# Two adapter layers with roles: orders and buffers of the first pair, of the changes of phase, of the left-overs and of the last pair

## The chip, the cores and the metric

The kernel runs on one core of one Trainium2 chip. The metric is the device time of one execution in microseconds (us), shown for several runs by its median. The profile is that of one further execution.

A core has a matrix engine (TensorE, PE in the profile; its weight loads are PEld), VectorE (DVE), ScalarE (ACT), GpSimd (POOL) and SyncE (SP), which here only issues transfers. Each engine works through its own list of instructions in order. Transfers between the main memory and the on-chip memory run on 16 DMA engines; they are issued from the list of SP or of ACT. TensorE writes into PSUM banks, which the other engines read.

## The reference

128 samples of 128 rows and 1024 columns (`x`) each have a role, drawn as 1 or 2 of three. Two layers follow one another, each with a set of weights for each role:

```python
h = jnp.einsum('bsh,bhk->bsk', hidden_states, W_down[role]) + b_down[role][:, None, :]
h = jax.nn.gelu(h, approximate=False)
u = jnp.einsum('bsk,bkh->bsh', h, W_up[role]) + b_up[role][:, None, :]
y = hidden_states + u
# mean and variance of y over its 1024 columns
return (y - mean) * jax.lax.rsqrt(var + LN_EPS) * gamma[role] + beta[role]
```

The inner width is 512. All data is float32.

## The kernel before

**Pairs, left-overs and phases.** At the start the kernel sorts the samples by role on the chip and takes two samples of one role as a pair: 63 pairs, and one item with the two samples that are left over, which may have different roles. There are four phases: down and up of the first layer (phases 0 and 1), down and up of the second (phases 2 and 3). A phase works through all 64 items; the left-over item comes after 31 pairs (`left_over_at`, L668). The results of a down phase (`hd`) and of the first layer (`mid`) go through the main memory.

**Seven products a pair.** The two samples of a pair stand above each other as a 2 by 2 block matrix, and so do the weights; the product is made from seven block products (`s1` to `s7`, L445 to L472) instead of eight. This takes sums of blocks of the activations (`winograd_sums`, L397, four instructions on GpSimd) and of the weights: T1 to T4. For phase 0 the weights are loaded as rows (`load_rows`, L142) and summed in place (`first_sum`, L162); for the other phases, class `Sums` makes the sums during phase 0 and stores them, and they are loaded block by block (B11, B21, T2, T1, T3, B22, T4) into the eight slots of `wall` as these come free. A left-over sample has the four products of the common method (`t1` to `t4`).

The products of one item add up in PSUM banks of three kinds, `b` (three banks), `a` (two) and `e` (three). Before the first product ACT writes the bias into a bank: the seed (`seeded`, L425). In a down phase ACT copies a bank into `h` (`begin`, L546), DVE adds another (`end`, L551) and ACT takes the GELU; the whole item is then stored by one transfer from ACT's list (`finish`, L557). In an up phase DVE adds the banks to `x` in place (L603, L608), the latter with a row sum; then `squares` (L624, on ACT with one small instruction on GpSimd), `scaled` (L634, DVE) and `stored` (L639) make the normalization and store the output from SP.

**Input of an item.** In a down phase each sample is loaded in four transfers of 128 KB (`quartered`, L383) and turned by a DVE transpose (L525) into the tile that TensorE reads. In an up phase `hq` comes in eight transfers of 64 KB (`load`, L569), and `x` of the residual in two of 512 KB (`load_rest`, L575).

**The order of the work.** All steps are put on a list with a time in slots by `at` (L661), and the instructions are issued in the order of these times; this fixes the order within each engine, and nothing more. An item takes seven slots, which is seven products. `base` is 7 times the item's number; the times of a class (`LOAD`, `REST`, `PREPARE`, `SEED`) and of its steps count from it. So the products of an item lie at 0, 2, ... 12, and those of two neighbours alternate. What a step waits for, beside the order, are data, buffers and the semaphores of the transfers, which are reused in turn.

**Buffers.** Tiles come from rings: `q` (four of 1024 columns: x of a down phase, `hq` and outputs of an up phase), `h` (two of 1024), `t` and `s` (three each). A new tile of a ring waits for the readers and transfers of the one that stood there before.

**The ends.** While the first weights are loaded, TensorE runs products of zeros (`zeros`, L269) into banks that nobody reads.

Of the kernel before, what the change touches and what calls it, by code (L numbers as in the profile page):

```python
# [19 lines left out]
P = 128  # L20
# [6 lines left out]
def kernel(  # L27
# [114 lines left out]
    def load_rows(k, place, engine, kind):  # L142
        w = layers[0][0]
        role = reg(role_of, place, [kind], R - 1)
        for q in range(NQ):
            src = w[ds(role, 1), ds(q * H // NQ + k * P, P), :]
            engine.dma_start(
                rows_of[k][ts(q, SQ), place].rearrange("p j h c -> p j (h c)"),
                src.rearrange("o (j i) c -> i (o j) c", i=SQ),
            )  # L150
# [123 lines left out]
    zeros("b")  # L274

# [80 lines left out]
    zeros("bbeee")  # L356
    for _ in range(4):
        zeros("bbb")
# [38 lines left out]
    def winograd_sums(dst, a):  # L397


        half = a.shape[2] // 2  # L400
        a11, a12, a21, a22 = (a[:, i, ts(k, half)] for i in range(2) for k in range(2))
        nc.gpsimd.tensor_tensor(dst[:, 1], a11, a21, ALU.subtract)  # L402
        nc.gpsimd.tensor_tensor(a21, a21, a22, ALU.add)
        nc.gpsimd.tensor_tensor(dst[:, 0], a21, a11, ALU.subtract)  # L404
        nc.gpsimd.tensor_tensor(dst[:, 2], a12, dst[:, 0], ALU.subtract)
# [26 lines left out]
    def item_products(item, cols):  # L432
# [9 lines left out]
        if n < NPAIR:  # L442
# [32 lines left out]
            times = (0, 2, 4, 1, 6.5, 6, 8) if item.early else range(0, 14, 2)  # L475
# [5 lines left out]
        for s in range(2):  # L481
# [18 lines left out]
            steps.append((2.5 * s - 4, lambda s=s, r=r: seed("b", (s, "b"), r)))  # L500
# [3 lines left out]
    class Down:  # L504
        LOAD, REST, PREPARE, SEED = -11.9, -11.8, -8.8, -4
# [6 lines left out]
        def load(self):  # L512
# [4 lines left out]
            quartered(self.xq, x_of(self.layer, self.n, ENG.SP))  # L517

        def load_rest(self):
            pass  # L520

        def prepare(self):
            self.a = flat("t", 3, "xT" + self.tag).rearrange("p (s j c) -> p s j c", s=2, c=P)
            for s in range(2):
# [3 lines left out]
                )  # L528
            self.sums = None
            if self.n < NPAIR:  # L530
# [3 lines left out]
                winograd_sums(self.sums, self.a)  # L534
# [5 lines left out]
        def first(self):  # L540
            self.h = flat("h", 2, "h" + self.tag, K * 2).rearrange("p (s n) -> p s n", s=2)

        def part(self, s, k):
            return self.h[:, s, ts(k, K // 2)]
# [12 lines left out]
        def finish(self):  # L557
            at = 12.5
            return [(at, lambda: nc.scalar.dma_start(hd[self.n].rearrange("s p n -> p s n"), self.h))]

    class Up:
        LOAD, REST, PREPARE, SEED = -11.5, -7, -5.5, -4
# [6 lines left out]
        def load(self):  # L569
            self.hq = flat("q", 4, "hq" + self.tag, H).rearrange(  # L570
                "p (s a c) -> p s a c", s=2, a=NQ
            )
            quartered([self.hq[:, s] for s in range(2)], [hd[self.n][s] for s in range(2)])
# [6 lines left out]
        def prepare(self):  # L580
            both = flat("s", 3, "hT" + self.tag, 1792)
            self.a = both[:, 0:1024].rearrange("p (s j c) -> p s j c", s=2, c=P)
            for s in range(2):
                nc.vector.transpose(  # L584
                    self.a[:, s].rearrange("p j (a t) -> p j a t", t=SQ),
                    self.hq[:, s].rearrange("p a (j i) -> p j a i", i=SQ),
# [6 lines left out]
            self.stat = small.tile([P, 2, 2], F32, tag="stat", name="stat" + self.tag)  # L593
# [11 lines left out]
        def end(self, s, k, ps):  # L605

            y = self.part(s, k)
            nc.vector.scalar_tensor_tensor(  # L608
# [4 lines left out]

        def finish(self):
            steps = []
# [54 lines left out]
    for k, ph in enumerate(phases):  # L670
        for m, n in enumerate(sequence):
# [4 lines left out]
            def load(box=box, ph=ph, n=n, kind=kind, m=m):  # L676
                item = box["item"] = kind(ph, n)
                item.early = ph is phases[0] and m == 0
                if ph is phases[2] and m == 0:
                    item.SEED = -0.6  # L680
                if m == left_over_at + 1:
                    item.SEED = -1.5
                item.load()

            at(base + kind.LOAD, load)
            at(base + kind.REST, lambda box=box: box["item"].load_rest())
# [54 lines left out]
    at(-12, lambda: load_bias([0]))  # L741
    at(-12, lambda: load_rows(0, 0, nc.scalar, ENG.Activation))
    at(-10, lambda: subtract(slice(0, 1)))
    at(-11, lambda: load_rows(1, 0, nc.sync, ENG.SP))
    for i, name in enumerate(("T1", "T2", "T3", "T4")):
        at(-8 + i / 10, lambda name=name: first_sum(name, 0))
# [50 lines left out]
```

## Time and profile before

| what | value |
|---|---|
| runs shown, median (lowest to highest) | 3194.6 us (3193.3 to 3203.4) |
| profiled execution, its own time | 3197.4 us |
| its span, first to last instruction | 3195.3 us |
| mean granted TensorE clock | 0.994 |
| TensorE busy | 3131.9 us (98%) |
| VectorE, ScalarE, GpSimd busy | 1772.8, 1200.4, 1791.7 us |
| moved by DMA | 642.9 MB, mean 201 GB/s |
| first real product starts at | 28.7 us |
| last pass of the last product starts at | 3177.0 us |
| first product of phases 1, 2 starts at | 811.9, 1617.8 us |

A line of a timeline has the start in us, the duration in us, the engine, the line of the kernel, the operation, the tile written and the tiles read, and in brackets how long the engine had been idle and what ended that. A float32 product of the kernel is recorded as two passes for each weight block, so that `x8` is one block product of a down phase (4 weight blocks) and `x4` one of an up phase (2 blocks). In tile names `b`, `a` and `e` are the banks, `d` and `u` the kind of phase: `bu` is a `b` bank of an up phase. `xTd`, `Sd` and `hTu` are turned activations and their sums.

### The profile page before, as it was taken

Reading aid. Unit: us, or ns where it says so; the run is one execution under the profiler, and the core shown is the slowest. Engines: PE = TensorE matmul, PEld = TensorE weight load, DVE = VectorE, ACT = ScalarE, POOL = GpSimd, SP = SyncE. Lnnn points to the kernel's source line nnn. Section 1 sums busy time; section 2 is a strip of 40 time slices with the busy share of each in tenths; the row PEclk is TensorE's granted clock in tenths of the full one; section 3 lists DMA queues with packets and bytes.
Section 4 is the critical chain, followed back from the end, with each engine's and each line's share of the span. In section 5 each row is a group of like instructions: output and inputs, shape, how many; then the busy total and the mean of one; then the engine's idle time right before and its main releaser. Section 6 shows DMA issues by size and latency. Waiting matters only on the chain. (4 is left out here: it accounts for less than half of the span.)

```text
span 3195.3 us, 43864 instructions
## 1 busy us (share of the span) xinstructions
PE 3131.9 (98%) x10824; PEld 2054.7 (64%) x10824; DVE 1772.8 (55%) x2783; ACT 1200.4 (38%) x2824; POOL 1791.7 (56%) x1399
## 2 busy tenths in 40 slices
PE   9999999999999999999989999999999999999997
PEld 6888888888534444444468888888884444444443
DVE  3533333334477777777743323233226777778877
ACT  1222222222345454545432222222224555454554
POOL 3544444444467776777754343443435777677775
PEclk9999999999999999999999999999999999999999
DMA  6776777777787666767796444544458766666664
GB/s 162 214 209 202 209 205 207 209 207 218 248 255 221 215 213 209 219 215 214 222 268 174 128 134 127 146 135 129 134 178 292 243 213 221 220 208 224 212 223 165
DMA packets 445506, 642.88 MB, mean 201 GB/s; under 512 B 46417, under 2 KB 316242, under 8 KB 445266
## 3 DMA queue, kind: packets, MB, share of 16 engines
q1 hardware_dynamic: 405986, 560.12, 59.6%
q10 hardware_dynamic: 39280, 79.96, 6.9%
q8 instruction: 102, 1.67, 0.2%
q14 instruction: 138, 1.13, 0.1%
HBM read 405.54 MB, written 234.36 MB: 200 GB/s over the span
## 5 line engine op out<-in xcount | busy, mean ns | idle before, releaser
L411 PE MATMUL bu<-wall,hTu 128*128 (+1 forms) x2048 | 929.9, 596 | 22.1 <-DVE xu L603 14.2
L411 PEld LDWEIGHTS bu<-wall,hTu 128*128 128x128 f32 x2048 | 386.3, 191 | 522.8 <-issue 426.2
L402 POOL TENSOR_TENSOR Sd<-xTd 128x512 f32<-128x512 f32 x126 | 168.6, 1338 | 842.0 <-DVE xTd L525 827.3
L632 POOL TENSOR_TENSOR varu<-varu,mhalf 128x1 f32<-128x1 f32 x256 | 334.8, 1308 | 414.6 <-ACT varu L631 367.0
L525 DVE STREAM_TRANSPOSE xTd<-xqd 128x1024 f32<-128x1024 f32 x256 | 307.9, 1230 | 438.8 <-PE bd L411 230.7
L411 PE MATMUL bd<-wall,xTd 128*128 (+1 forms) x2080 | 491.7, 380 | 7.8 <-DVE hd L551 5.2
L635 DVE SCALAR_TENSOR_TENSOR ou<-xu,meanu,tables 128x1024 f32<-128x1024 f32 x256 | 328.8, 1284 | 302.7 <-ACT ou L630 300.5
L411 PE MATMUL eu<-wall,hTu 128*128 (+1 forms) x1040 | 490.1, 594 | 4.1 <-DMA wall<-B 3.8
L411 PE MATMUL bd<-wall,Sd 128*128 (+1 forms) x2016 | 478.0, 380 | 4.4 <-ACT hd L547 4.4
L411 PEld LDWEIGHTS bd<-wall,xTd 128*128 128x128 f32 x2080 | 394.8, 190 | 66.2 <-DVE hd L551 7.3
L411 PEld LDWEIGHTS bd<-wall,Sd 128*128 128x128 f32 x2016 | 383.6, 190 | 59.4 <-POOL Sd L404 3.3
L411 PEld LDWEIGHTS eu<-wall,hTu 128*128 128x128 f32 x1040 | 198.0, 191 | 253.9 <-issue 240.6
L552 ACT ACTIVATE hd<-hd 128x256 f32<-128x256 f32 x382 | 157.2, 416 | 490.0 <-DVE hd L551 489.7
L626 ACT ACTIVATE partu<-statu 128x2 f32<-128x2 f32 x256 | 52.1, 203 | 759.4 <-DVE xu L608 759.4
L643 POOL TENSOR_TENSOR ou<-ou,tables 128x1024 f32<-128x1024 f32 x128 | 301.3, 2354 | 1.2 <-DMA hqu<-hd 0.9
L630 ACT ACTIVATE ou<-xu,meanu 128x1024 f32<-128x1024 f32 x256 | 294.0, 1148 | 19.1 <-DMA mid<-ou 4.2
L411 PE MATMUL ed<-wall,xTd 128*128 (+1 forms) x1072 | 252.9, 379 | 0.0
L402 POOL TENSOR_TENSOR hTu<-hTu 128x256 f32<-128x256 f32 x126 | 204.3, 1621 | 79.5 <-DVE hTu L584 77.7
L411 PE MATMUL ed<-wall,Sd 128*128 (+1 forms) x1008 | 238.1, 379 | 0.0
L411 PE MATMUL ad<-wall,xTd 128*128 (+1 forms) x1008 | 238.1, 379 | 0.0
L411 PE MATMUL au<-wall,hTu 128*128 (+1 forms) x504 | 236.8, 592 | 0.0
L411 PEld LDWEIGHTS ed<-wall,xTd 128*128 128x128 f32 x1072 | 203.7, 190 | 28.1 <-ACT ou L630 0.2
(96 smaller groups left out, 3348.6 us busy)
## 6 DMA issues: line engine op xcount, KB each, us to landing
xqd<-in_x_dram SPq DMA_DIRECT2D x512, 128.0 KB, 3.0
hd<-hd ACTq DMA_DIRECT2D x128, 512.0 KB, 2.8
hqu<-hd SPq DMA_DIRECT2D x1024, 64.0 KB, 4.1
xu<-in_x_dram SPq DMA_DIRECT2D x128, 512.0 KB, 5.3
mid<-ou SPq DMA_DIRECT2D x128, 512.0 KB, 5.2
xqd<-mid SPq DMA_DIRECT2D x512, 128.0 KB, 3.5
xu<-mid SPq DMA_DIRECT2D x128, 512.0 KB, 5.8
out_dram<-ou SPq DMA_DIRECT2D x128, 512.0 KB, 4.9
```

Of the source, the lines that this page charges most:

```text
L402: nc.gpsimd.tensor_tensor(dst[:, 1], a11, a21, ALU.subtract)
L411: nc.tensor.matmul(ps[:, 0:cols], a[:, j], w.rhs(r, j, cols), start=start and j == 0, stop=j == n - 1, skip_group_check=True,)
L525: nc.vector.transpose(self.a[:, s].rearrange("p j (a t) -> p j a t", t=SQ), self.xq[s].rearrange("p a (j i) -> p j a i", i=SQ),)
L552: nc.scalar.activation(y, y, AF.Gelu)
L626: nc.scalar.mul(part, self.stat[:, s], -1.0 / H)
L630: nc.scalar.activation(box["o"], self.x[:, s], AF.Square, bias=m, accum_out=v)
L632: nc.gpsimd.tensor_tensor(v, v, mhalf[:, 0:1], ALU.pow)
L635: nc.vector.scalar_tensor_tensor(box["o"], self.x[:, s], box["m"][:, 0:1], row(self.ph.gamma), ALU.add, ALU.mult)
L643: nc.gpsimd.tensor_tensor(o, o, row(self.ph.beta), ALU.add)
```

## The change

- **First pair.** Sample by sample, x is loaded at slots -30 and -27. The first two quadrants of the first weight rows are issued by ACT, the other two by SP; of the second rows, SP issues two quadrants after the second sample and ACT two at slot -3, after the seeds. T1 is summed between the two transposes, and three of the four activation sums are made by DVE. The second and third product change places. There are 9 products of zeros instead of 18.
- **x in phase 0** is loaded 19 slots ahead of `base` (17.4 for the fourth item) instead of 11.9. Phase 2 keeps its times.
- **h by sample.** Two rings `h0` and `h1` of two tiles each, and one store for each sample, at slots 10.7 and 12.5 instead of one at 12.5.
- **hq.** The first three items of an up phase load it at slot -16 instead of -11.5, into the ring `q`; the later ones load it at -11.5 as before, into `h0` and `h1`.
- **Left-overs.** The second sample's seed and the next pair's seed move from slot -1.5 to -1.65.
- **Last pair.** Mean and variance come from DVE's `bn_stats` and `bn_aggr`, and the output is stored in four pieces of 256 KB from SP and ACT.

```diff
-    def load_rows(k, place, engine, kind):
+    def load_rows(k, place, engine, kind, quadrants=range(NQ)):
         w = layers[0][0]
         role = reg(role_of, place, [kind], R - 1)
-        for q in range(NQ):
+        for q in quadrants:
             src = w[ds(role, 1), ds(q * H // NQ + k * P, P), :]
...
-    zeros("b")
     iota_row, iota_col, ones, upper = f32(B), f32(1), f32(B), f32(B)
...
     place = gathered("place", wide_place, onehot)
-    zeros("bbeee")
-    for _ in range(4):
-        zeros("bbb")
+    zeros("bbbeeebbb")
...
-    def winograd_sums(dst, a):
+    def winograd_sums(dst, a, engine=nc.gpsimd):
...
         a11, a12, a21, a22 = (a[:, i, ts(k, half)] for i in range(2) for k in range(2))
-        nc.gpsimd.tensor_tensor(dst[:, 1], a11, a21, ALU.subtract)
-        nc.gpsimd.tensor_tensor(a21, a21, a22, ALU.add)
-        nc.gpsimd.tensor_tensor(dst[:, 0], a21, a11, ALU.subtract)
+        engine.tensor_tensor(dst[:, 1], a11, a21, ALU.subtract)
+        engine.tensor_tensor(a21, a21, a22, ALU.add)
+        engine.tensor_tensor(dst[:, 0], a21, a11, ALU.subtract)
         nc.gpsimd.tensor_tensor(dst[:, 2], a12, dst[:, 0], ALU.subtract)
...
-            times = (0, 2, 4, 1, 6.5, 6, 8) if item.early else range(0, 14, 2)
+            times = (0, 1, 4, 2, 6.5, 6, 8) if item.early else range(0, 14, 2)
             steps = list(zip(times, (s1, s2, s3, s4, s5, s6, s7)))
...
             steps += [(1.75 * s + 3.5 * i, f) for i, f in enumerate((t1, t2, t3, t4))]
-            steps.append((2.5 * s - 4, lambda s=s, r=r: seed("b", (s, "b"), r)))
+            steps.append(((-4, -1.65)[s], lambda s=s, r=r: seed("b", (s, "b"), r)))
             steps.append((1.5 * s + 0.5, lambda s=s, r=r: seed("e", (s, "e"), r)))
...
     class Down:
-        LOAD, REST, PREPARE, SEED = -11.9, -11.8, -8.8, -4
+        LOAD, PREPARE, SEED = -11.9, -8.8, -4
...
             ]
-            quartered(self.xq, x_of(self.layer, self.n, ENG.SP))
+            self.srcs = x_of(self.layer, self.n, ENG.SP)
+            quartered(self.xq[0:1], self.srcs[0:1])
         def load_rest(self):
-            pass
+            quartered(self.xq[1:2], self.srcs[1:2])
...
                 )
+                if s == 0 and self.early:
+                    first_sum("T1", 0)
             self.sums = None
...
                 )
-                winograd_sums(self.sums, self.a)
+                winograd_sums(self.sums, self.a, nc.vector if self.early else nc.gpsimd)
             set_places(self, [ENG.PE, ENG.Activation])
...
         def first(self):
-            self.h = flat("h", 2, "h" + self.tag, K * 2).rearrange("p (s n) -> p s n", s=2)
+            self.h = [flat(f"h{s}", 2, f"h{self.tag}_{s}", K) for s in range(2)]
         def part(self, s, k):
-            return self.h[:, s, ts(k, K // 2)]
+            return self.h[s][:, ts(k, K // 2)]
...
         def finish(self):
-            at = 12.5
-            return [(at, lambda: nc.scalar.dma_start(hd[self.n].rearrange("s p n -> p s n"), self.h))]
+            return [
+                (t, lambda s=s: nc.scalar.dma_start(hd[self.n][s], self.h[s]))
+                for s, t in enumerate((10.7, 12.5))
+            ]
     class Up:
-        LOAD, REST, PREPARE, SEED = -11.5, -7, -5.5, -4
+        LOAD, PREPARE, SEED = -11.5, -5.5, -4
...
         def load(self):
-            self.hq = flat("q", 4, "hq" + self.tag, H).rearrange(
-                "p (s a c) -> p s a c", s=2, a=NQ
-            )
-            quartered([self.hq[:, s] for s in range(2)], [hd[self.n][s] for s in range(2)])
+            if self.m < 3:
+                hq = flat("q", 4, "hq" + self.tag, H)
+                self.hq = [hq[:, ts(s, K)] for s in range(2)]
+            else:
+                self.hq = [flat(f"h{s}", 2, f"hq{self.tag}_{s}", K) for s in range(2)]
+            self.hq = [t.rearrange("p (a c) -> p a c", a=NQ) for t in self.hq]
+            quartered(self.hq, [hd[self.n][s] for s in range(2)])
...
                     self.a[:, s].rearrange("p j (a t) -> p j a t", t=SQ),
-                    self.hq[:, s].rearrange("p a (j i) -> p j a i", i=SQ),
+                    self.hq[s].rearrange("p a (j i) -> p j a i", i=SQ),
                 )
...
             set_places(self, [ENG.PE, ENG.DVE, ENG.Pool, ENG.Activation])
-            self.stat = small.tile([P, 2, 2], F32, tag="stat", name="stat" + self.tag)
+            if self.last:
+                self.stat = const.tile([P, 2, 2, 6], F32, name="last_stat")
+            else:
+                self.stat = small.tile([P, 2, 2], F32, tag="stat", name="stat" + self.tag)
...
             y = self.part(s, k)
+            if self.last:
+                nc.vector.tensor_tensor(y, ps, y, ALU.add)
+                nc.vector.bn_stats(self.stat[:, s, k], y)
+                return
             nc.vector.scalar_tensor_tensor(
...
+        def finish_last(self):
+            mv = [const.tile([P, 3], F32, name=f"last_mv{s}") for s in range(2)]
+            o = [flat("q", 4, f"o{self.tag}_{s}", H) for s in range(2)]
+            out_row = lambda s: out[ds(self.out_at[s], 1)].rearrange("o s h -> (o s) h")
+            row = lambda t, s, cols: t[:, ds(self.places[s], 1), cols].rearrange("p o n -> p (o n)")
+            self.out_at = [reg(perm, 2 * self.n + s, [ENG.SP, ENG.Activation], B - 1) for s in range(2)]
+            left, right, both = slice(0, H // 2), slice(H // 2, H), slice(0, H)
+            def total(s):
+                nc.vector.bn_aggr(mv[s][:, 0:2], self.stat[:, s])
+                v = mv[s][:, 2:3]
+                nc.vector.tensor_scalar(v, mv[s][:, 1:2], LN_EPS, None, ALU.add)
+                nc.gpsimd.tensor_tensor(v, v, mhalf[:, 0:1], ALU.pow)
+            def scaled(s):
+                nc.vector.scalar_tensor_tensor(
+                    o[s], self.x[:, s], mv[s][:, 0:1], row(self.ph.gamma, s, both), ALU.subtract, ALU.mult
+                )
+            def stored(s, cols, queue):
+                y, v = o[s][:, cols], mv[s][:, 2:3]
+                nc.vector.scalar_tensor_tensor(y, y, v, row(self.ph.beta, s, cols), ALU.mult, ALU.add)
+                queue.dma_start(out_row(s)[:, cols], y)
+            def stored_beside():
+                y, v = o[0][:, left], mv[0][:, 2:3]
+                nc.scalar.mul(y, y, v)
+                nc.gpsimd.tensor_tensor(y, y, row(self.ph.beta, 0, left), ALU.add)
+                nc.scalar.dma_start(out_row(0)[:, left], y)
+            return [
+                (10.2, lambda: total(0)),
+                (12.2, lambda: total(1)),
+                (12.4, lambda: scaled(0)),
+                (12.5, lambda: scaled(1)),
+                (12.6, lambda: stored(1, left, nc.sync)),
+                (12.7, lambda: stored(1, right, nc.sync)),
+                (12.8, stored_beside),
+                (12.9, lambda: stored(0, right, nc.sync)),
+            ]
         def finish(self):
+            if self.last:
+                return self.finish_last()
             steps = []
...
                 item = box["item"] = kind(ph, n)
+                item.m = m
                 item.early = ph is phases[0] and m == 0
+                item.last = ph is phases[-1] and m == NI - 1
                 if ph is phases[2] and m == 0:
...
                 if m == left_over_at + 1:
-                    item.SEED = -1.5
+                    item.SEED = -1.65
                 item.load()
-            at(base + kind.LOAD, load)
-            at(base + kind.REST, lambda box=box: box["item"].load_rest())
+            if ph.up:
+                first, rest = (-16 if m < 3 else -11.5), -7
+            elif k == 0:
+                first = {0: -30, 1: -19, 2: -19, 3: -17.4}.get(m, -19)
+                rest = -27 if m == 0 else first + 0.05
+            else:
+                first, rest = -11.9, -11.8
+            at(base + first, load)
+            at(base + rest, lambda box=box: box["item"].load_rest())
...
     ph.bias, load_bias, subtract = bias_table(ph.vectors[0], 2)
-    at(-12, lambda: load_bias([0]))
-    at(-12, lambda: load_rows(0, 0, nc.scalar, ENG.Activation))
-    at(-10, lambda: subtract(slice(0, 1)))
-    at(-11, lambda: load_rows(1, 0, nc.sync, ENG.SP))
-    for i, name in enumerate(("T1", "T2", "T3", "T4")):
-        at(-8 + i / 10, lambda name=name: first_sum(name, 0))
+    at(-29, lambda: load_bias([0]))
+    at(-29, lambda: load_rows(0, 0, nc.scalar, ENG.Activation, (0, 1)))
+    at(-28, lambda: load_rows(0, 0, nc.sync, ENG.SP, (2, 3)))
+    at(-27, lambda: subtract(slice(0, 1)))
+    at(-26, lambda: load_rows(1, 0, nc.sync, ENG.SP, (2, 3)))
+    at(-3, lambda: load_rows(1, 0, nc.scalar, ENG.Activation, (0, 1)))
+    for i, name in enumerate(("T2", "T3", "T4")):
+        at(-2.5 + i / 10, lambda name=name: first_sum(name, 0))
     at(14.7, lambda: load_bias(range(1, R)))
...
     for k in range(1, R):
```

## The prediction

> **What bounds the kernel now.** I read the busy table first: TensorE (PE) is busy for 98% of the span, so only the other 2% and the ends can be won. Then PE's busy time by stretch. Columns: stretch, length, PE busy (instructions), granted clock, DMA share, GB/s.
>
> ```profile
> 0.00:28.60 28.60, 21.31 (x48) 1.00 0.60 124
> 28.60:800.00 771.40, 762.26 (x3514) 1.00 0.74 207
> 800.00:840.00 40.00, 36.23 (x118) 0.91 0.89 292
> 840.00:1200.00 360.00, 353.58 (x817) 1.00 0.72 224
> 1200.00:1222.00 22.00, 19.28 (x41) 0.92 0.70 216
> ...
> 1596.00:1620.00 24.00, 14.78 (x31) 0.79 0.93 272
> ...
> 2770.00:2790.00 20.00, 16.15 (x38) 1.00 0.59 198
> ...
> 3178.00:3195.00 17.00, 0.00 (x0) 0.56 0.30 124
> ```
>
> Modelled ends hide part of each gap, so I count by starts: a 256-column pass starts 0.216 us after the last, a 512-column one 0.431 us. The excess of the starts over that, in gaps above 0.06 us, sums to 56.2 us: 13.1 in phase 0 (28.6 to 800), 6.6 at the change to phase 1 (at 833), 9.6 from 840 to 1200, 4.9 at phase 1's left-overs (1206, 1219), 1.0 up to 1596, 12.7 at the change to phase 2, 1.3 in phase 2, 1.3 before 2770, 4.4 at phase 3's left-overs, 1.4 at the end. Outside stand 28.7 us before the first real product and 18.3 us after the start of the last pass (3177.0). Next, the waits of phase 0 by engine (us in total, times, longest):
>
> ```profile
> PE bd L411 <- DVE hd L551: 5.2, 4, 2.1
> PE bd L411 <- ACT hd L547: 3.8, 2, 2.4
> ```
>
> ```profile
> DVE xTd L525 <- DMA xqd<-in_x_dram: 163.7, 50, 11.2
> ```
>
> ```profile
> SPq L388 <- DMA hd<-hd: 195.0, 37, 9.2
> ```
>
> PE waits for VectorE's (DVE's) additions, which queue behind transposes that wait for x; SP issued that x late because it waited for an h store. The DMA issues reuse eight semaphores in rotation, so a load waits for a transfer some eight issues earlier, whichever queue sent it. The two waits on ScalarE (ACT) are copies into an h buffer whose store had not landed (7.75 us before 120.73).
>
> The timelines at the left-over, the start and the tail:
>
> ```profile
> 1203.38 0.68 DVE L608 SCALAR_TENSOR_TENSOR xu<-bu,xu 128x512 f32<-128x512 f32 x1
> ...
> 1206.19 0.58 ACT L429 COPY bu<-tables 128x512 f32 x1
> ...
> 1206.82 3.66 PE L411 MATMUL bu<-wall,hTu 128*128 x4 [2.33 <-ACT bu L429]
> ```
>
> ```profile
> 28.69 1.89 PE L411 MATMUL bd<-wall,xTd 128*128 128x256 f32 x8
> 30.41 1.89 PE L411 MATMUL ed<-wall,xTd 128*128 128x256 f32 x8
> 32.14 1.89 PE L411 MATMUL ad<-wall,xTd 128*128 128x256 f32 x8
> ```
>
> ```profile
> 3175.46 3.27 DVE L645 SCALAR_TENSOR_TENSOR ou<-ou,varu,tables 128x1024 f32<-128x1024 f32 x1
> ...
> 3182.41 0.68 DVE L608 SCALAR_TENSOR_TENSOR xu<-bu,xu 128x512 f32<-128x512 f32 x1
> ...
> 3186.70 3.35 DVE L645 SCALAR_TENSOR_TENSOR ou<-ou,varu,tables 128x1024 f32<-128x1024 f32 x1 [0.44 <-POOL varu L632]
> ```
>
> **What the Trainium skill says.** "PSUM — Partial Sum Buffer", Engine vs sequencer instructions: the queues of ACT, DVE and GpSimd (POOL) are strictly first in, first out. The trace agrees: the seed at 1206.19 needs a bank free at about 1204.0, yet runs after ACT's square chain. "TensorE: Matmul & The Clock Gate", What's actually happening: PE falls to half clock after an idle window of about 3.4 us. Here 2.50 and 2.60 us of gap were followed by half-rate passes (0.43 us instead of 0.216 at 121), 2.44 us was not; the measured edge decides. "SBUF — State Buffer", SBUF: two separate sides: DVE and POOL lock a shared port against each other. It agrees: L645 takes 3.27 us beside POOL's 2.34 us addition, 1.28 elsewhere.
>
> **The change part by part** (gain positive).
>
> *Start: -0.6 us, between +1.5 and -6.* Landings of the first transfers run in issue order, 0.6 us per 128 KB of x, 1.2 us per 256 KB of weight rows; the fourth part of x and the bias have landed by 16.9. The second product after the change needs B21, so all rows: still to land are 4.8 (first rows) + 2.4 (second sample) + 4.8 (second rows) us, hence 28.9 at best. Before, the last of these rows landed at 29.6: bandwidth, not order. The last two row loads now stand on ACT behind the seeds, which wait for the bias subtraction and for the warm-up bank (about 20.1), so one or two x loads of 0.6 us may go ahead: 29.5. Nine warm-up products instead of 17 here (0.86 us each, the first two twice that) end at about 21.7, the first product runs at about 22.5, then PE idles 5 us and runs the next eight passes at half rate: 1.7 us lost. 29.5 - 1.73 + 1.7 = 29.4 stands against 28.7: 0.7 lost, less 0.1 for VectorE's faster sums (three at about 0.7 for 1.3 to 2.1). If the semaphores put these rows behind the third pair's x, they land near 35: the -6.
>
> *x 19 slots ahead, h by sample: +11.5, between +6 and +13.* A slot is 1.73 us. x goes from 3.1 slots (5.4 us) before its transposes to 10.2 slots (17.6 us); its eight issues and their landing take 8 to 11 us. Its buffers come free at slot -22.8, 3.8 before. The stalls of late x (81.8, 108.1, 211.6, 284.7, 577.1) are 6.8 us. The first sample's store goes from slot 12.5 to 10.7, 3.1 us earlier, and the next write into it waits for that half alone: the stalls of late h (121.2, 442.1, 794.5) are 6.2 us. I keep an eighth of both. The 128 extra stores cost ACT 0.4 us each, beside its 62% idle time; without that cover they would cost 51 us. Phase 2 keeps its x times and gains +0.8 from h alone (0 to 1.3).
>
> *Change to phase 1: +5.6, between 0 and +6.6.* The block PE waited for at 833 was issued at 826.9 behind eight hq loads begun at 815.9. Those now stand 4.5 slots earlier, ahead of the second pair's x. SP may issue the block as soon as its slot's last reader is done, about 819; at a 5.9 us landing it is there before 829. I leave 1.0 us.
>
> *840 to 1200: +1.0, between -4 and +4.* Role weights, hq, x and stores fill 0.9 of the DMA engines here; the times of hq from the fourth pair on stay. Its new buffers end a wait for an output's landing, but the semaphores hold SP at much the same place.
>
> *Left-overs: +8.6, between +6 and +9.3.* The seeds move from slot -1.5 to -1.65, across the squares at -1.6 (the following pair's cross its own at 5.4 in the same way). The bank is free at 1204.0; a seed of 0.58 then ends at about 1204.65, against PE free at 1204.33: 0.3 us stays, no half clock follows, nor the stall at 1219. That is 4.9 - 0.3, and 4.4 - 0.4 in phase 3. The squares move 0.6 us later; ACT's next idle time hides it.
>
> *Change to phase 2: 0, between -3 and +8.* Here ACT's square waits for an output store issued at 1592.86 to land at 1600.6, then transposes wait for x to 1605.1. Neither the reuse of that buffer nor these slots change.
>
> *Tail: +3.3, between +1 and +5.* No square pass (1.15 + 0.29 + 0.20) stays in the last pair. bn_stats has no row; nearest is L608 at 0.68, bounds 0.3 and 1.4, taken 0.7. DVE is still held by L645 to 3178.7; then add and stats of two blocks (4 x 0.7), two totals (2 x 0.4): 3182.3. Two scalings (2 x 1.28): 3184.9; three half stores (3 x 0.69) and POOL's half addition in the way (1.2): 3188.2, against 3190.05 for L645. The last piece is half of 512 KB, which took 5.2 us at the end; with three others just ahead I take 3.8: 3192.0 against 3195.3.
>
> Sum: -0.6 + 11.5 + 0.8 + 5.6 + 1.0 + 8.6 + 0 + 3.3 = 30.2. The span of 3195.3 becomes 3165.1; that execution took 3197.4, 2.1 more, and becomes 3167.2. The median of the runs is 2.8 below it, which gives 3164.4. I say 3165.
>
> **Rivals.**
> - *Given back in the loaded first half, 0.20.* DMA runs at 207 GB/s in phase 0 and at 280 after 820; SP's in-order queue still waits for h stores, now two a pair. If half of phase 0's stalls stay (6.5) and the change to phase 1 only moves its lateness on (1), the gain is -1 + 6.5 + 1 + 8.6 + 2.5 = 17.6: 3177. Against it: 17.6 us of lead is longer than any wait seen for x.
> - *The start loses its 6 us, 0.10:* 3170. For it: the rotation of semaphores; against it: ACT's issue comes long before the third pair's can go, since that waits for transposes of 24.8.
> - *More than the named stalls, 0.08:* the change to phase 2 or the stretch from 840 falls too, some 12 us more: 3153. Against it: their slots stand.
> - *Slower, 0.04.* The store at slot 10.7 makes ACT wait for a semaphore of an SP load not landed, and the copies behind it hold PE. It decides where each of 128 Down items loses 30.2/128 = 0.24 us; at 0.35 us it gives 3209. Against it: ACT's waits for h now need late stores, and loads move earlier.
>
> **How the numbers follow.** The forecast has 0.58 with its own range 3158 to 3171. Adding the start and most of the two neighbours gives 3152 to 3179. A time within 0.3% (9.6 us) cannot be told from no change. Faster takes all cases but the slower one and a corner of the first rival: 0.93; same 0.03, slower 0.04.
>
> **What would show it.** DVE's wait for x in phase 0 falls below 50 us and PE's waits there to 2 us; the wait for a block near 833 is gone; at both left-overs the seed precedes the squares; the 7 us wait near 1600 stays; PE shows a 5 us gap after the first product; DVE's last instruction ends about 3.5 us before the span. A stall that recurs item by item on ACT ahead of the h store would make it wrong.

## The result, and the profile after

The kernel with the change takes 3195.6 us (median of 14 runs, 3190.6 to 3205.9), the kernel before on the same chip 3200.2 us (14 runs, 3193.3 to 3204.9). The ratio is 0.999 (95% interval 0.9982 to 0.9999): a gain of 0.1%, less than the 0.3% within which the prediction called times equal, where the forecast was 30 us less. The profiled execution took 3195.3 us with a span of 3193.5 us, 1.8 us less than before.

TensorE by stretch, with the columns of the table in the prediction:

```profile
...
28.60:800.00 771.40, 758.58 (x3484) 0.99 0.75 206
800.00:840.00 40.00, 38.46 (x141) 1.00 0.83 287
...
1200.00:1222.00 22.00, 20.07 (x46) 1.00 0.66 209
...
2355.00:2370.00 15.00, 11.60 (x48) 0.89 0.97 269
2770.00:2790.00 20.00, 18.69 (x44) 1.00 0.56 179
```

The stretches at 800, 1200 and 2770 are fuller, as forecast. Phase 0 is emptier, and at 2355 TensorE now stands still where it did not before. Counted by starts, as in the prediction, term by term. The excess is the time by which TensorE's passes start later than at full rate. The start is the first product's start plus the excess up to 60 us; the tail runs from the start of the last pass to the end of the span.

| term | before | after | gain | forecast |
|---|---|---|---|---|
| start | 28.7 | 29.9 | -1.2 | -0.6 |
| phase 0, 60 to 800 | 13.1 | 16.5 | -3.5 | +11.5 |
| change to phase 1 | 6.6 | 1.8 | +4.8 | +5.6 |
| 842 to 1196 | 9.6 | 6.4 | +3.2 | +1.0 |
| both left-overs | 9.3 | 4.2 | +5.0 | +8.6 |
| change to phase 2 | 12.7 | 13.3 | -0.5 | 0 |
| phase 2 to the change to phase 3 | 1.3 | 5.1 | -3.8 | +0.8 |
| tail | 18.3 | 18.9 | -0.6 | +3.3 |
| rest of the up phases | 3.6 | 5.3 | -1.6 | 0 |

The gains come to 1.8 us, and the spans differ by as much.

**Phase 0.** The waits from 60 to 800 us (us in total, times, longest), of TensorE, VectorE, ScalarE and SP in the kernel after:

```profile
PE bd L407 <- DVE hd L550: 11.0, 8, 2.4
...
DVE xTd L522 <- DMA xqd<-in_x_dram: 97.5, 42, 4.8
...
ACT hd L546 <- DMA hd<-hd: 11.2, 9, 2.2
...
SPq L384 <- DMA hd<-hd: 152.3, 42, 9.5
SPq L212 <- DMA hd<-hd: 94.5, 26, 6.0
SPq L203 <- DMA hd<-hd: 81.7, 11, 9.6
```

Two changes here did what they say. ScalarE's waits for an h store fell to 11.2 us, and the longest wait for x from 11.2 us to 4.8. In the kernel before, ScalarE's row was:

```profile
ACT hd L547 <- DMA hd<-hd: 128.8, 43, 7.8
```

But TensorE waits longer for VectorE than before (11.0 us against 5.2), and SP still stands for h stores, 328 us in these three rows. The loads and stores that waited have no data in common with h: L384 loads x here, L203 loads weights and L212 stores their sums.

One such time, SP's list (a group's duration runs from its first issue to the end of its last, waits included), VectorE's and TensorE's:

```profile
192.23 10.52 SPq L203 DMA_DIRECT2D tables<-in_L_cond_W_up_dram  x4
203.66 18.54 SPq L384 DMA_DIRECT2D xqd<-in_x_dram  x16
...
217.08 1.25 DVE L522 STREAM_TRANSPOSE xTd<-xqd 128x1024 f32<-128x1024 f32 x1 [4.12 <-DMA xqd<-in_x_dram]
...
222.58 1.99 PE L407 MATMUL bd<-wall,xTd 128*128 128x256 f32 x8 [1.19 <-DVE hd L550]
```

The trace also names the completion semaphore of each transfer. These are issues of SP and ACT in that time, in order of time:

```
192.23 SP  weights  105
196.43 ACT h store  107
199.39 ACT h store  109
201.42 SP  weights  109   waited for 109
201.93 SP  weights  110
202.43 SP  weights  111
203.66 SP  x        112
204.18 SP  x        101
204.70 SP  x        105
208.52 ACT h store  107
211.48 ACT h store  108
214.40 SP  x        107   waited for 107
```

Eight semaphores (101, 105, 107 to 112) are reused over both engines' transfers, and which transfer takes which is fixed beforehand: the load that waited for 109 did not take 110 or 111, whose transfers had landed by 194.0. ACT issues its stores when the GELUs are done. The weight load after 192.23 stands for 8.7 us because its semaphore is the one that an h store, issued only at 199.39 and landed at 201.40, takes first. The x load at 214.40 waits in the same way for the store of 208.52, which landed at 214.38, and everything on SP behind them waits too. The transposes come late, VectorE's addition comes behind them, and TensorE loses 1.35 us. Such gaps recur at steps of about 74 us (222.6, 296.2, 370.4, then 518.8, 592.8, 738.8), about the time of one job of weight sums (42 slots).

**Change to phase 3.** ScalarE's list and TensorE's:

```profile
2355.45 6.56 ACTq L119 DMA_DIRECT2D tables<-in_L_cond_ln_w_dram  x3
2362.05 0.37 ACT L546 COPY hd<-bd 128x256 f32<-128x256 f32 x1 [9.38 <-DMA tables<-in_L_cond_ln_w_dram]
...
2362.56 2.05 PE L407 MATMUL bd<-wall,Sd 128*128 x4 [3.40 <-ACT hd L546]
```

The third load of the scale waited on ACT for the semaphore of a bias load issued 7 us earlier. The copy that frees a bank stood behind it, TensorE waited 3.40 us and then ran at half rate.

**Left-over.** ScalarE and VectorE at the first one:

```profile
1200.71 0.59 ACT L425 COPY bu<-tables 128x512 f32 x1 [1.63 <-DVE xu L620]
1201.80 1.15 ACT L687 ACTIVATE ou<-xu,meanu 128x1024 f32<-128x1024 f32 x1
...
1209.97 1.15 ACT L687 ACTIVATE ou<-xu,meanu 128x1024 f32<-128x1024 f32 x1
...
1211.25 1.28 DVE L692 SCALAR_TENSOR_TENSOR ou<-xu,meanu,tables 128x1024 f32<-128x1024 f32 x1 [1.88 <-ACT ou L687]
1212.45 0.68 DVE L620 SCALAR_TENSOR_TENSOR xu<-bu,xu 128x512 f32<-128x512 f32 x1
...
1213.18 0.59 ACT L425 COPY bu<-tables 128x512 f32 x1 [1.63 <-DVE xu L620]
```

The second sample's seed now runs at 1200.71, ahead of the squares of 1201.80, and of the stall at 1206, with its half rate, 0.5 us are left. The next pair's seed at 1213.18 is ahead of its squares too, but it has no bank: the bank is freed by VectorE's addition of 1212.45, which stands behind L692, and L692 waits 1.88 us for the squares of 1209.97. No seed held these squares up, for ScalarE had stood idle for 4.01 us before them. TensorE, no longer late from the first stall, is there before the bank and stands 1.9 us. In the kernel before it stood 0.6 us at this place. At the second left-over the same stall was 1.9 us before and is 1.5 us after.

**Tail.** VectorE and SP:

```profile
3178.72 0.69 DVE L618 BATCH_NORM_STATS2 last_stat<-xu 128x6 f32<-128x512 f32 x1
...
3182.41 2.89 DVE L649 SCALAR_TENSOR_TENSOR ou<-ou,last_mv,tables 128x512 f32<-128x512 f32 x3
...
3184.00 6.87 SPq L650 DMA_DIRECT2D out_dram<-ou  x3
```

Counted from the start of the last pass, VectorE is done after 10.7 us, 2.3 us sooner than before. But the four stores, three from SP and one from ACT, went out at 3184.00, 3186.11, 3188.36 (ACT's) and 3190.54. The first three landed at 3186.01, 3188.12 and 3190.41: each store went out only after the one before had landed.

### The profile page after: what moved, and what is told of

Same layout as the page of the kernel before. It is cut to its first block, busy times and chain, and to the rows that moved or that the text cites. A ratio compares the mean times of both kernels' runs of the same rounds, so it can differ in the third digit from the quotient of the medians.

```text
span 3193.5 us, 43475 instructions
## 1 busy us (share of the span) xinstructions
PE 3123.4 (98%) x10806; PEld 2054.9 (64%) x10806; DVE 1762.3 (55%) x2792; ACT 1199.2 (38%) x2814; POOL 1767.4 (55%) x1396
## 5 line engine op out<-in xcount | busy, mean ns | idle before, releaser
L692 DVE SCALAR_TENSOR_TENSOR ou<-xu,meanu,tables 128x1024 f32<-128x1024 f32 x254 | 326.2, 1284 | 317.6 <-ACT ou L687 317.6
L407 PEld LDWEIGHTS ed<-wall,xTd 128*128 128x128 f32 x1072 | 204.7, 191 | 28.7 <-ACT ou L687 0.2
```

Source lines behind the costliest of these rows:

```text
L407: nc.tensor.matmul(ps[:, 0:cols], a[:, j], w.rhs(r, j, cols), start=start and j == 0, stop=j == n - 1, skip_group_check=True,)
L692: nc.vector.scalar_tensor_tensor(box["o"], self.x[:, s], box["m"][:, 0:1], row(self.ph.gamma), ALU.add, ALU.mult)
```

## The experiments

Theory R: in phase 0, SP's loads stand behind the other engine's stores, and x's lead is not what lacks. Its rivals: x or h is simply late (L), or new costs elsewhere eat a gain that phase 0 had. The runs come from several chips, on which the kernel before had medians from 3196.2 to 3202.0 us, so it is the ratios that compare kernels, not the times. Excess in phase 0 and what was varied, as measured, each excess in one execution:

| kernel | base | h store | x ahead, slots | excess 60 to 800 us | ratio to before |
|---|---|---|---|---|---|
| before | | pair, ACT | 11.9 | 13.1 | 1 |
| x ahead alone | before | pair, ACT | 19 | 23.2 | 1.0052 |
| h on SP alone | before | pair, SP | 11.9 | 8.7 | 1.0015 |
| after | | sample, ACT | 19 | 16.5 | 0.999 |
| x late | after | sample, ACT | 11.9 | 9.0 | 0.9964 |
| h on SP | after | sample, SP | 19 | 5.2 | 0.9952 |
| both | after | sample, SP | 11.9 | 7.3 | 0.9971 |
| with tables on SP | combined | sample, SP | 19 | 0.3 | 0.9936 |
| the same, x late | combined | sample, SP | 11.9 | 0.4 | 0.9934 |

Three more kernels below (hq late, two stores, the old order) have the phase 0 of the kernel after: 15.0, 14.6 and 16.1 us. Differences of 2 us between single executions mean nothing.

**h's stores on SP.**

```diff
-                (t, lambda s=s: nc.scalar.dma_start(hd[self.n][s], self.h[s]))
+                (t, lambda s=s: nc.sync.dma_start(hd[self.n][s], self.h[s]))
```

> The changed kernel with one edit: both h stores are issued by SP instead of ACT, at the same slots. Theory R (x is late because the eight DMA semaphores go round over the transfers of both queues, so that SP's loads wait for h stores that ACT issues much later): in SP's own list an x load stands 1.7 slots or more before the next store, nothing waits across queues, and the excess of PE's starts in phase 0 (16.5 us after 36 us) falls below 5 us; the run is 9 to 14 us shorter than the changed kernel's, 3182 to 3187 us. Theory B (the DMA engines are too busy for x in time): the excess stays at 13 to 20 us and the time within 4 us. Theory Q (the ring of x's buffers holds the loads back): as B.

Measured: 3189.1 us, ratio 0.9952 (0.9939 to 0.9965), span 3188.3. Phase 0's excess fell from 16.5 to 5.2 us, just above what theory R expected. SP's waits in phase 0 and what is left of TensorE's:

```profile
SPq L558 <- ACT bd L425: 106.5, 41, 7.1
...
PE bd L407 <- ACT hd L546: 3.0, 3, 2.5
```

SP still waits, but at the store itself, for ScalarE. The loads behind it are in the order of SP's own issues, and they wait 0.2 us in all for h stores, against 344 us over all of SP's lines before the edit. This is theory R. The edit also takes 118 issues of 0.33 us off ACT, but TensorE's waits for ScalarE in phase 0 had been 1.5 us, too little to give 11. Of the 5.2 us left, 4.2 are one stall at 773 us, where ScalarE stood behind its own loads of tables. Elsewhere the stall of the change to phase 3 grew from 5.1 to 7.9 us.

**x as before.**

```diff
-                first = {0: -30, 1: -19, 2: -19, 3: -17.4}.get(m, -19)
+                first = {0: -30, 1: -19, 2: -19, 3: -17.4}.get(m, -11.9)
```

> The changed kernel with x of phase 0 back at slot -11.9 from the fifth item on. Theory R: the slot of the load isn't what sets its time, the store that it waits for is; the excess in phase 0 stays at 12 to 21 us and the time within 4 us of the changed kernel. Theory L (19 slots do help, and without them it would be worse by what h by sample costs): the excess rises to 27 us or more, the time by 10 us.

Measured: 3193.0 us, ratio 0.9964 (0.9952 to 0.9976). Phase 0's excess is 9.0 us, less than after's 16.5: the longer lead makes it worse, which neither theory had. VectorE's waits for x do grow back (97.5 to 149.2 us), but TensorE's for VectorE shrink (11.0 to 4.5):

```profile
PE bd L407 <- DVE hd L550: 4.5, 6, 1.9
...
DVE xTd L522 <- DMA xqd<-in_x_dram: 149.2, 47, 10.9
```

**The kernel before with x 19 slots ahead**, nothing else:

```diff
-            at(base + kind.LOAD, load)
+            at(base + (-19 if k == 0 and m > 3 else kind.LOAD), load)
```

> The kernel before with one edit: x of phase 0 is loaded 19 slots ahead from the fifth item on. The runs so far say that this makes phase 0 worse beside h stored by sample (16.5, 14.6 and 15.0 us of excess with it, 9.0 without). Theory R (SP's place is set by the h stores that it waits for, and loads that stand earlier in its list take the slots of the rotation ahead of them, so nothing is gained): the excess of phase 0 stays between 11 and 20 us against 13.1. Theory L (19 slots help when h is stored at once): it falls to 8 us or less.

Measured: 3215.6 us, ratio 1.0052 (1.0037 to 1.0066); phase 0's excess rose from 13.1 to 23.2 us, above even theory R's 11 to 20, and one more gap of 4.4 us, which ends at 60.7, stands just ahead of the stretch. By itself this part of the change costs time, as above. TensorE's waits in phase 0, 9.0 us before, and SP's for h stores at its loads of x, 188.5 us before:

```profile
PE bd L411 <- DVE hd L551: 12.0, 9, 4.2
PE bd L411 <- ACT hd L547: 5.8, 3, 2.1
```

```profile
SPq L388 <- DMA hd<-hd: 222.7, 38, 13.3
```

The sum of SP's waits for h stores does not tell what they cost: over all its lines it is 320 us in the kernel before, 336 here, 344 in after and 332 with x late, whose excess is the smallest of the four.

**h on SP and x late together** (the two edits above).

> The changed kernel with the h stores issued by SP and x of phase 0 back at slot -11.9 from the fifth item on: the fourth corner of slots by queues. Theory R: with one list nothing waits across queues, now the lead decides; with 3.1 slots of lead and an h store ahead of it in the list x comes late at many items, the excess of phase 0 rises from 5.2 to 12 us or more. If the lead doesn't matter there either: 3 to 8 us.

Measured: 3189.0 us, ratio 0.9971 (0.9961 to 0.998), phase 0's excess 7.3 us, where theory R expected 12 or more. The lead does not decide here either: 7.2 of the 7.3 us are one wait for ScalarE and the half rate behind it, at the same place as in the run with h on SP. ScalarE stood there behind its own load of a table:

```profile
773.69 0.37 ACT L546 COPY hd<-bd 128x256 f32<-128x256 f32 x1 [9.88 <-DMA tables<-in_L_cond_gamma_dram]
```

**The kernel before with its h store on SP.**

```diff
-            return [(at, lambda: nc.scalar.dma_start(hd[self.n].rearrange("s p n -> p s n"), self.h))]
+            return [(at, lambda: nc.sync.dma_start(hd[self.n].rearrange("s p n -> p s n"), self.h))]
```

> The kernel before, with one edit: h's one store per pair goes to SP's queue instead of ACT's. Theory R (the loads of phase 0 stand behind stores of the other queue, x's lead is not what lacks): the excess of phase 0, 13.1 us before, falls to 3 to 8, SP's waits for hd<-hd there go from 320 us to under 20, the span is 3186 to 3191. Theory L (x is simply asked for too late, at 11.9 slots ahead): the store on SP, which waits for the last gelu, pushes x back further; phase 0 stays at 11 or more and the span at 3193 or more.

Measured: 3201.0 us, ratio 1.0015 (1.0008 to 1.0022), span 3197.6. Phase 0's excess is 8.7 us, just above the 3 to 8 that theory R expected, but the span is not the 3186 to 3191 that it expected. SP's waits for h stores are gone (0.5 us), but ScalarE's are not (112.0 us, 35 times), and now they are what TensorE feels; its waits in phase 0:

```profile
PE bd L411 <- ACT hd L547: 6.3, 9, 1.4
```

With one store a pair, h goes out late and the next copy into its buffer waits for it. What this execution won in phase 0 it lost in small pieces elsewhere (1.3 us at the change to phase 1, 1.8 in phase 2, about 2 between 2372 and 2765), and the kernel as a whole is not faster than before. The two parts help different waits: h by sample those for the buffer, its store on SP those of the loads. That both are needed rests on few executions: with x late, the store alone leaves 8.7 us, h by sample alone 9.0, and both together 7.3, nearly all of it the stall at the table loads.

**The change to phase 3: hq late there.**

```diff
-                first, rest = (-16 if m < 3 else -11.5), -7
+                first, rest = (-16 if m < 3 and k == 1 else -11.5), -7
```

> The changed kernel with hq of phase 3's first three items back at slot -11.5; phase 1 keeps -16. If the early hq loads are what puts the gamma loads on ACT behind a semaphore, the stall near 2362 (5.1 us with its half clock) falls to 1.3 us or less, as in the kernel before. If the two stores of h are the cause, it stays at 4 to 6 us.

Measured: 3202.0 us, ratio 1.0002 (0.9993 to 1.001). The wait for the scale table is gone, but ScalarE stalls 6 us later, and the excess there is still 5.0 us. ScalarE and SP:

```profile
2359.64 0.34 SPq L791 DMA_DIRECT2D wall<-B  x1
...
2368.08 0.34 ACTq L558 DMA_DIRECT2D hd<-hd  x1
2368.46 0.37 ACT L546 COPY hd<-bd 128x256 f32<-128x256 f32 x1 [4.73 <-DMA wall<-B]
```

The h store on ACT waited for the semaphore of a block load of SP, issued at 2359.64. This is the wait of the prediction's slower rival. It is rare: with x late, an h store at 788 us also waited 3.4 us for a load of x. Here moving the loads only moved the place where a turn falls badly.

**Two stores at the end** in place of four, both from SP, with the scaling and shifting all on VectorE (the diff shows the order of the steps alone).

```diff
...
-                (12.5, lambda: scaled(1)),
-                (12.6, lambda: stored(1, left, nc.sync)),
-                (12.7, lambda: stored(1, right, nc.sync)),
-                (12.8, stored_beside),
-                (12.9, lambda: stored(0, right, nc.sync)),
+                (12.5, lambda: stored(0)),
+                (12.6, lambda: scaled(1)),
+                (12.7, lambda: stored(1)),
```

> The changed kernel with the last pair's output in two stores of 512 KB, one for each sample, both from SP, the scaling and shifting all on DVE. Theory S (each store to the output waits until the one before has landed, 2.1 us for 256 KB against 2.6 us for 512 KB): the first store goes at about 3182.5, the second at 3185.2, it lands at 3187.9 and the span ends 18.8 - 4.5 = 14.3 us after the start of PE's last pass. Rival (the pieces aren't the cause, the landing of the last data is): the tail stays at 18 to 19.5 us.

Measured: 3194.7 us, ratio 0.998 (0.997 to 0.9989), span 3192.2. The tail fell from 18.9 to 14.3 us. VectorE and SP:

```profile
3185.84 3.04 SPq L650 DMA_DIRECT2D out_dram<-ou  x2
...
3187.11 1.28 DVE L649 SCALAR_TENSOR_TENSOR ou<-ou,last_mv,tables 128x1024 f32<-128x1024 f32 x1
```

VectorE ends 10.5 us after the start of the last pass, as with four pieces (10.7), yet the whole tail is 4.6 us shorter: the first store flies while the second sample is computed, and only one store has to wait for a landing at the end. In this execution other gaps were longer, so that its span is only 1.3 us below after's; by the ratios the two kernels can't be told apart.

**The order of the first pair's products as before.**

```diff
-            times = (0, 1, 4, 2, 6.5, 6, 8) if item.early else range(0, 14, 2)
+            times = (0, 2, 4, 1, 6.5, 6, 8) if item.early else range(0, 14, 2)
```

> The changed kernel with the first pair's second and third product in the order of the kernel before (T1 second, B21 third). If the 5 us gap before the second product is only waiting for B21's rows, the T1 product fills part of it: it can run once DVE has the sum of the second sample, near 26.8, B21 at about 30; the excess of PE's starts up to 60 us falls from 7.7 to 5 to 6.5 us. If the gap has another cause (T1 or the seeds late too) it stays at 7.5 or more.

Measured: 3192.2 us, ratio 0.9982 (0.9972 to 0.9992). The first product starts at 21.0 and the first pair's excess is 6.3 us, together 27.3. In after it was 29.9, and in the five other kernels that keep after's first pair (the experiments above but the two on the kernel before), 28.7 to 29.4. TensorE's second product, after and then with this order:

```profile
28.95 3.75 PE L407 MATMUL ad<-wall,xTd 128*128 128x256 f32 x8 [4.91 <-DMA wall<-in_L_cond_W_down_dram]
```

```profile
26.07 3.75 PE L407 MATMUL ed<-wall,xTd 128*128 128x256 f32 x8 [3.07 <-DVE xTd L399]
```

The old order waits for the sums, which come before the last weight rows. The gain of 1.4 to 2.6 us is seen in the profile; by the medians of the runs alone it can't be told from nothing.

**Combined**: h on SP, two stores, the old order, and all tables but the first bias loaded from SP:

```diff
-                r = reg(role_of, k, [ENG.Activation], R - 1)
-                nc.scalar.dma_start(t[:, k], v[ds(r, 1), :].to_broadcast((P, n)))
+                first = places == [0]
+                r = reg(role_of, k, [ENG.Activation if first else ENG.SP], R - 1)
+                queue = nc.scalar if first else nc.sync
+                queue.dma_start(t[:, k], v[ds(r, 1), :].to_broadcast((P, n)))
```

> The changed kernel with four edits: h stores on SP; bias, gamma and beta tables on SP but for the first bias; T1 second in the first pair; the last output in two stores. Theory R carried on: ACT then waits for no transfer's semaphore in order to issue one, so the stall near 2356 (7.9 us with h on SP) falls below 2 us; phase 0 stays near 5 us, the first pair near 6, the tail near 14.3 us. Against the changed kernel's span of 3193.5: -11 -2 -4.5 -3.5 = 3172, time 3174 to 3180. If the tables on SP delay loads as much as they free ACT, the stall stays and the time is 3181 to 3186.

Measured: 3175.7 us, ratio 0.9936 (0.9924 to 0.9949), span 3172.2. Phase 0 has 0.3 us left, the change to phase 3 has 0.1, the tail is 14.3. But the change to phase 2 grew from 13.3 to 20.5 us; what TensorE waited for there, beside the wait of about 7 us that is there before and after (7.7 here, 7.4 in after):

```profile
PE bd L409 <- ACT bd L427: 8.5, 1, 8.5
```

**The same with x late** (11.9 slots, the edit of "x as before").

> The combined kernel (h and most tables on SP, the order of the first pair as before, two stores at the end; phase 0's excess 0.3 us, span 3172.2) with x asked for 11.9 slots ahead as before. Theory S (the 19-slot lead cost time only through the order of two queues' transfers): with nearly all transfers on one queue neither lead stalls; phase 0 stays below 1.5 us, span 3172 plus or minus 2. Theory L (the lead is worth its 11 us once nothing else is in its way): phase 0 rises by 4 us or more, span 3176 or more.

Measured: 3175.2 us, ratio 0.9934 (0.992 to 0.9947), phase 0's excess 0.4 us. VectorE's waits for x in phase 0 were 2.0 us in the combined kernel and are 97.3 here, as long in total as in after, and TensorE feels none of it:

```profile
DVE xTd L524 <- DMA xqd<-in_x_dram: 97.3, 25, 8.7
```

So with nearly all transfers issued by SP the lead is worth nothing, and it costs nothing: theory S of the expectation, not L.

**Phase 2's first bias back on ACT.**

```diff
-                first = places == [0]
+                first = places == [0] or (which == 0 and n == K)
```

> The combined kernel with phase 2's first bias load back on ACT's queue, all else as there. If the 7 us that the change to phase 2 lost there (excess 13.3 to 20.5) come from that load standing on SP behind the transposes of the pair: the excess there returns to 12.5 to 14.5 and the span is 3165 to 3167. If not (the stores of mid hold it): over 18, span 3170 or more.

Measured: 3170.6 us, ratio 0.9924 (0.991 to 0.9937), span 3162.5. The span is that of the fastest of five runs. The change to phase 2 has 14.7 us: the 6 us came from that bias. Phase 0 is full, in the columns of the first table:

```profile
28.60:800.00 771.40, 771.40 (x3569) 1.00 0.78 211
```

**And phase 2's first x three slots earlier.**

```diff
-                first, rest = -11.9, -11.8
+                first, rest = (-15, -14.95) if k == 2 and m == 0 else (-11.9, -11.8)
```

> As the run before it, and the two x loads of phase 2's first pair are asked for at slots -15 and -14.95 instead of -11.9 and -11.8. If the change to phase 2 is held by those sixteen transposing loads standing ahead of the stores of mid in SP's order: its excess falls from about 13 to 6 to 9 us, span 3158 to 3162. If it is held by the stores of mid themselves, which the loads must wait for: 12 or more, span 3165 or more.

Measured: 3167.4 us, ratio 0.9907 (0.9892 to 0.9922), span 3166.9, change to phase 2 14.7 us. The 6 to 9 us expected if those loads were in the way did not come, so they are not what holds that change; the intervals of this kernel and the one above overlap. Both are faster than the kernel before by 0.6 to 1.1%, which the change as made is not.

## Why the prediction was wrong

Point by point, by its own terms:

- **x ahead and h by sample, +11.5: the failed step.** It took "from 3.1 slots to 10.2 slots before its transposes" as lead in time. The list's order gives no such lead while SP stands wherever a semaphore's turn falls to an h store that ACT has yet to issue. The prediction named these turns and SP's waits for h stores, and still let them cost nothing; its first rival gave half of phase 0 back, and all of it and more was. Measured: -3.5. The half of the step on h held (ScalarE's waits for h stores 128.8 to 11.2 us). The half on x failed in sign: by itself it cost 10.1 us of excess in the kernel before, and 5.6 to 7.6 beside h by sample. With h by sample stored from SP, phase 0 has 5.2 us left, 4.2 of them at the table loads, and 0.3 with the tables there too. *Why* the longer lead is worse than the shorter one with two issuing engines is not settled; that it is not worse where SP issues nearly all was shown.
- **Change to phase 1, +5.6: right** (4.8). The wait of 3.8 us for a block near 833 is gone; 1.5 us for another block at 828.6 are left, where 1.0 was forecast. **842 to 1196, +1.0:** 3.2, inside its bounds; what brought the other two was not tried.
- **Left-overs, +8.6: right for the first seed, mis-sized as a whole** (5.0). At the second sample's seed the first left-over keeps 0.5 us, with 0.3 forecast. The step that failed is "nor the stall at 1219": the next pair's seed lacks not its turn on ScalarE but a bank, which an addition of VectorE frees late, behind L692 and its wait for squares. It costs 1.9 us at 1213.8 and 1.5 at the second left-over.
- **Phase 2, +0.8: wrong** (-3.8 with the change to phase 3). No term asked what the three hq items moved to slot -16 would collide with on ACT's list there. That the stall at the scale table comes from them, and that moving them back only moves it, is shown.
- **Change to phase 2, 0: right** (-0.5). The 7 us wait near 1600 stayed, 7.4 us.
- **Start, -0.6:** -1.2, with the 5 us gap after the first product (4.91) and the half rate that were forecast.
- **Tail, +3.3: failed** (-0.6). "With three others just ahead I take 3.8": the pieces are not ahead, they wait for one another, and the last goes out 5.2 us after VectorE's end. The computation was sized well (bn_stats 0.69 us for the 0.7 taken; VectorE done 10.7 us after the start of the last pass, for the 11.2 forecast).
- **Of the rivals**, that of the given-back gain named the right mechanism and half its size; its 17.6 us would still have been a gain. The slower one's wait is seen to hold TensorE in the experiment with hq late; the stall that recurs in after is SP's, not ScalarE's.

Against the forecast, phase 0 is 15.0 us short, phase 2 with the change to phase 3 4.6, the tail 3.9 and the left-overs 3.6. Of what was said to show it, the seeds, 833, 1600 and the 5 us gap came true; VectorE's waits for x (97.5 us, not below 50), TensorE's in phase 0 (12.5, not 2) and the end of VectorE (8.2 us before the span, not 3.5) did not.

About as much as the forecast 30 us can be had from this kernel: by the ratios, the kernel with the bias on ACT gains 24 us and the last one 30. But what they add to the change comes mostly from the queue on which things are stored and loaded and from the two stores at the end, not from the times at which loads are asked for. That the amounts agree is chance.

## What to carry to other kernels

Before you move a load ahead, read what its issuing engine waits for: if it is a transfer of another engine's list, with no data in common, an earlier place in the list need not win anything (here it cost time), and what helped was to issue both from one list. Put a transfer that waits for a computation where nothing urgent stands behind it: h's stores did no harm on SP, while one bias load there cost 6 us. Stores to one output that wait for each other were better few and early than small: two took 4.6 us less than four.

## What the runs showed of the hardware

- Moving phase 0's stores of h from ACT to SP did not lower the rate of the transfers: 206 GB/s in phase 0 after, 211 in the kernel with the bias on ACT, where SP issues nearly all. This agrees with the Trainium skill, "DMA: Bandwidth & Descriptors", Issuing engines are not separate DMA queues: transfers issued by several engines run on the same 16 DMA engines, and a second issuer saves only issuing time. What the second issuer cost here, by the shared semaphores, is the larger side: 11 us of phase 0.
- At the end, stores to the output took 2.0 us each from issue to landing for 256 KB, one after the other, and 2.6 us for 512 KB: half the size saved a fifth of the time.
- The half clock did not follow the length of the gap alone. After a gap of 2.55 us by starts TensorE went on at full rate (1.99 us for eight passes), after one of 2.11 us it ran at half rate (3.54 us):

```profile
96.36 1.99 PE L407 MATMUL bd<-wall,xTd 128*128 128x256 f32 x8 [2.38 <-DVE hd L550]
...
122.74 3.54 PE L407 MATMUL bd<-wall,xTd 128*128 128x256 f32 x8 [1.94 <-DVE hd L550]
```

The Trainium skill, "TensorE: Matmul & The Clock Gate", What's actually happening, has TensorE at half clock after at least one idle window of about 3.4 us, and the window running freely. That it runs freely fits both gaps; that a whole idle window is needed does not, for a gap of 2.11 us was enough here.
